# Three depthwise 3x3 convolutions of a four-layer kernel: four taps on TensorE and five on VectorE, in pieces of 448 pixels

## The chip, the core and the metric

The kernel runs on one NeuronCore of a Trainium2 chip. A core has several engines with instruction queues of their own: TensorE (PE, matrix products into the PSUM banks), VectorE (DVE), ScalarE (ACT), GpSimd (POOL) and SyncE (SP, which issues DMA transfers here). [...] SBUF is the working memory with 128 partitions, and PSUM is the memory that TensorE writes to, in banks of 512 fp32 numbers for each partition.

The metric is the device time of one execution in microseconds (us). The time before is 17090.54 us, the median of three runs (17080.33 to 17101.61).

## What is computed

A batch of 4 images of 96 channels and 56 x 56 pixels passes four layers in a row, each with a group norm ahead and a residual around it: attention, a selective scan in eight directions, a top-k aggregation over windows, and a state-space layer in four directions with a convolutional bottleneck. Depthwise 3x3 convolutions occur in three places, one in layer 1 and two in layer 3:

```python
# layer 1, DI = 192 channels
xz = einsum('bchw,dc->bdhw', x, w_in);  xc, z = split(xz, 2, axis=1)
xc = conv_general_dilated(xc, conv_w, (1, 1), 'SAME', feature_group_count=DI)
xc = silu(xc + conv_b)
xs = cross_scan(xc)        # rows, columns, diagonals, antidiagonals, and each reversed

# layer 3, E = 192 channels
xi, z = split(einsum('bchw,oc->bohw', x, in_proj_w), 2, axis=1)
xi = silu(conv2d(xi, conv_w, conv_b, groups=E, pad=1))
...
t = relu(bn(conv2d(u, c1_w, c1_b)))                           # 1x1, 192 -> 384
t = relu(bn(conv2d(t, c2_w, c2_b, groups=2 * E, pad=1)))      # depthwise
t = conv2d(t, c3_w, c3_b)                                     # 1x1, 384 -> 96
s = sigmoid(relu(t.mean((2, 3)) @ se1_w.T + se1_b) @ se2_w.T + se2_b)
return t + t * s
```

A depthwise convolution gives each output pixel as a sum of nine products: nine neighbours of the pixel in its own channel, each by a weight of that channel. One of the nine products, over all pixels of a tile, is called a tap below. Everything is fp32.

## The kernel before

**Tiles.** A map of 56 x 56 has 3136 pixels (`L`), cut into `NCH` = 7 chunks of `CH` = 448 pixels, that is 8 rows. A convolution works on a tile of 128 partitions. In the input stages of layers 1 and 3 a tile holds 64 channels of two images; with `NPAIR` = 2 pairs of images and `NB` = 3 blocks of 64 channels there are 6 tiles in a stage. In the bottleneck a tile holds 128 of the 384 channels of one image, `NM` = 3 tiles for each of the 4 images.

**The convolution before.** `depthwise` (L326 to L333) reads a map with a border of zeros, `xp` or `t1` of 58 x 58, whose border four GpSimd memsets write for every tile (`pad_border`, L319). VectorE runs one scaling (L331) and eight multiply-adds (L333) over all 3136 pixels, one after another, with the sum `cv` in SBUF.

**Layer 1's input, `into_scan` (L252 to L317).** For each pair: load image x (L273, queue SP, one buffer), `group_norm` (L88 to L110: statistics by VectorE, two tiny products by TensorE, a root by ScalarE, the scaling by VectorE), store the normalised image (L276), the same for the second image. Then for each tile j: for each chunk two matmuls, one for each image (L282), and a ScalarE copy into the map (L293); `depthwise`; Silu over the whole tile by ScalarE (L299); a doubled copy `dup` of the tile, one half by ScalarE (L302) and one by GpSimd (L303); four orders of the pixels for the scans: rows (stored as it is, L307), columns (copied by ScalarE, L311), diagonals and antidiagonals (copied by GpSimd, L313 and L315), each stored by SP's queue (L316).

**Layer 3's input, `into_layer3` (L846 to L895).** The same, with two orders only: rows and columns (ScalarE's copy, L888), stored in halves of 64 partitions.

**Layer 3's end, `layer3` (L1246 on).** For each image `gathered` loads the normalised image `xn` (L1285) and, for 7 groups of 448 pixels, the four scan results `y0` to `y3` (L1293 and L1299). VectorE adds them (L1303, L1304) and normalises them (`norm_rows`, L596), multiplies by a matmul's result z (L1309, L1310), and TensorE transposes them (L1314) into `g` (ScalarE's copy, L1318). Then `bottleneck`: for each tile, the c1 matmuls (L1330, two for each chunk), Relu by ScalarE into the map (L1334), `depthwise`, Relu over the whole tile into `t2` (L1341). When all three tiles are there: the c3 matmuls (L1351, three for each chunk), ScalarE's output (L1352) with sums for the mean, the two small products of the gate (L1356 to L1366), and seven output products (L1370, VectorE), each stored by GpSimd's queue (L1371).

**What sets the order.** The tile framework schedules instructions by their dependencies, and each engine runs its own queue in that order. In these three stages nothing is ordered by hand before the change. Other stages (`scans`, `cumulative`) use `in_order` (L52 to L67), which ties every instruction of a block to the one written ahead of it on the same engine. The two pools of an image's gather (`ob`, `os`) are closed before those of its bottleneck (`tb`, `t1`, `ts`) open, so both use the same stretch of SBUF, and a load of the next gather has to wait until whatever lies at its address in the bottleneck has been read for the last time.

Of the kernel before, what the change touches and what calls it, by code (L numbers as in the profile page):

```python
# [9 lines left out]
F32 = mybir.dt.float32  # L10
AF = mybir.ActivationFunctionType
# [20 lines left out]
def view(ap, offset, dims):  # L32

    return bass.AP(ap.tensor, ap.offset + offset, [ap.ap[0], *dims])


def flat(t):
    return t.rearrange("p a b -> p (a b)")
# [31 lines left out]
class Net:  # L70
# [180 lines left out]

    def into_scan(self, xin, dram, orders):  # L252
# [3 lines left out]
        us = []  # L256
        xs = [dram.tile([C, L], F32, name=f"l1x{b}") for b in range(B)]
        with ExitStack() as cx:
# [8 lines left out]
            for pr in range(NPAIR):  # L267
                u = [dram.tile([128, NB, L], F32, name=f"l1u{pr}{o}") for o in orders]
                us.append(dict(zip(orders, u)))
                xn = []  # L270
                for half in range(2):
                    x = s1.tile([C, L], F32, name="x")
                    nc.sync.dma_start(x, xin[2 * pr + half])  # L273
                    xh = s1.tile([C, L], F32, name=f"xn{half}")
                    self.group_norm(x, xh, ss, ps, "p")
                    nc.sync.dma_start(xs[2 * pr + half], xh)  # L276
                    xn.append(xh)

                def project(col, c):
                    p = ps.tile([128, 512], F32, name="p")  # L280
                    for half in range(2):
                        nc.tensor.matmul(  # L282
                            p[64 * half : 64 * half + 64, :CH], win[:, col : col + 64],
                            xn[half][:, c * CH : (c + 1) * CH], start=True, stop=True,
                        )
                    return p

                for j in range(NB):
                    xp = sp.tile([128, H + 2, W + 2], F32, name="xp")
                    self.pad_border(xp)  # L290
                    for c in range(NCH):
                        p = project(64 * j, c)
                        nc.scalar.copy(  # L293
                            xp[:, 1 + 8 * c : 9 + 8 * c, 1 : W + 1],
                            p[:, :CH].rearrange("p (h w) -> p h w", w=W),
                        )
                    cv = sp.tile([128, H, W], F32, name="cv")
                    self.depthwise(cv, xp, cw[:, j, :])
                    nc.scalar.activation(cv, cv, AF.Silu, bias=cb[:, j : j + 1])  # L299

                    dup = sp.tile([128, H, 2 * W], F32, name="dup")
                    nc.scalar.copy(dup[:, :, 0:W], cv)  # L302
                    nc.gpsimd.tensor_copy(dup[:, :, W : 2 * W], cv)  # L303
                    for o in orders:
                        dst = us[pr][o][:, j, :]
                        if o == "rows":
                            nc.sync.dma_start(dst, flat(cv))  # L307
                            continue
                        t = sp.tile([128, W, H], F32, name="t")
                        if o == "cols":  # L310
                            nc.scalar.copy(t, view(cv, 0, [[1, W], [W, H]]))  # L311
                        elif o == "diag":
                            nc.gpsimd.tensor_copy(t, view(dup, 0, [[1, W], [2 * W + 1, H]]))  # L313
                        else:
                            nc.gpsimd.tensor_copy(t, view(dup, W, [[1, W], [2 * W - 1, H]]))  # L315
                        nc.sync.dma_start(dst, flat(t))  # L316
        return us, xs  # L317

    def pad_border(self, xp):  # L319
        nc = self.nc  # L320
        nc.gpsimd.memset(xp[:, 0, :], 0.0)
        nc.gpsimd.memset(xp[:, H + 1, :], 0.0)
        nc.gpsimd.memset(xp[:, 1 : H + 1, 0:1], 0.0)
        nc.gpsimd.memset(xp[:, 1 : H + 1, W + 1 : W + 2], 0.0)

    def depthwise(self, out, xp, w):  # L326
        nc = self.nc
        for k in range(9):
            src = xp[:, k // 3 : k // 3 + H, k % 3 : k % 3 + W]
            if k == 0:  # L330
                nc.vector.tensor_scalar(out, src, w[:, 0:1], None, ALU.mult)  # L331
            else:
                nc.vector.scalar_tensor_tensor(out, src, w[:, k : k + 1], out, ALU.mult, ALU.add)  # L333
# [512 lines left out]
    def into_layer3(self, xin, dram):  # L846
# [4 lines left out]
        with ExitStack() as cx:  # L851
# [8 lines left out]
            for pr in range(NPAIR):  # L860
                xn = []
                for half in range(2):
                    b = 2 * pr + half
                    x = s1.tile([C, L], F32, name="x")
                    nc.sync.dma_start(x, xin[b])
                    xh = s1.tile([C, L], F32, name=f"xn{half}")
                    self.group_norm(x, xh, ss, ps, "p")
                    nc.sync.dma_start(xs[b], xh)
                    xn.append(xh)
                for j in range(NB):  # L870
                    xp = sp.tile([128, H + 2, W + 2], F32, name="xp")
                    self.pad_border(xp)
                    for c in range(NCH):
                        p = ps.tile([128, 512], F32, name="p")
                        for half in range(2):
                            nc.tensor.matmul(
                                p[64 * half : 64 * half + 64, :CH], win[:, 64 * j : 64 * j + 64],
                                xn[half][:, c * CH : (c + 1) * CH], start=True, stop=True,
                            )
                        nc.scalar.copy(  # L880
                            xp[:, 1 + 8 * c : 9 + 8 * c, 1 : W + 1],
                            p[:, :CH].rearrange("p (h w) -> p h w", w=W),
                        )
                    cv = sp.tile([128, H, W], F32, name="cv")
                    self.depthwise(cv, xp, cw[:, j, :])
                    nc.scalar.activation(cv, cv, AF.Silu, bias=cb[:, j : j + 1])
                    t = sp.tile([128, W, H], F32, name="t")
                    nc.scalar.copy(t, view(cv, 0, [[1, W], [W, H]]))  # L888
                    for half in range(2):
                        hs = slice(64 * half, 64 * half + 64)  # L890
                        for o, a in (("rows", cv), ("cols", t)):
                            nc.sync.dma_start(
                                us[o][2 * pr + half, 64 * j : 64 * j + 64, :], flat(a[hs])
                            )
# [350 lines left out]
    def layer3(self, xin, xout, dram):  # L1245
# [4 lines left out]
        with ExitStack() as cx:  # L1250
            wp = cx.enter_context(tc.tile_pool(name="ow", bufs=1))
            ga = cx.enter_context(tc.tile_pool(name="og", bufs=1))
            ps = cx.enter_context(tc.tile_pool(name="op", bufs=4, space=PSUM))
            psz = cx.enter_context(tc.tile_pool(name="oz", bufs=2, space=PSUM))
# [65 lines left out]
            def bottleneck(b, g, sp, s1, ss):  # L1320
# [3 lines left out]
                for m in range(NM):  # L1324
# [200 lines left out]
```

## Time and profile before

| what | us |
|---|---|
| median of 3 runs | 17090.54 |
| profiled execution, device time | 17096.45 |
| its span (first to last instruction on the core) | 17094.7 |
| VectorE busy | 13981.4 (82%) |
| TensorE busy | 13251.9 (78%) |
| ScalarE busy | 12242.0 (72%) |
| GpSimd busy | 7703.0 (45%) |

A profile is one execution, recorded instruction by instruction. These busy shares are averages over stages of different kind: layer 0 runs to about 2619 us, layer 1's input to 2956, its scans and merging and all of layer 2 to 11101, layer 3's input to 11394, its scans to about 16300, and then the four gathers and bottlenecks. How full the engines are where the convolutions run shows only in windows of time.

How to read its lines. A group of instructions: line, engine, operation, output tile <- input tiles, shapes, number | busy us, mean ns of one | idle time of the engine just before them, and what ended it. The chain that ended last is followed back from the last instruction, at each step to what released it, so what is on it sets the time. In a table of windows each row is a stretch of time, with the busy time of each engine and the number of its instructions, then the granted TensorE clock as a share of full speed, and the share of time in which the DMA engines were busy. A timeline gives start and duration of single instructions, and in square brackets how long the engine had been idle and what released it. PEld is TensorE's weight load; a "q" behind an engine's name is its sequencer. A matmul of fp32 numbers shows as two records.

The first half of a convolution in the bottleneck of the last image is short enough to be read through (timeline of TensorE and ScalarE): the c1 matmuls come in one block, and ScalarE follows each chunk.

```profile
16959.02 17.49 PE L1330 MATMUL pn<-g,w_l_c 96*128 96x448 f32 x43
...
16961.93 0.72 ACT L1334 ACTIVATE t<-pn,bn_sh,bn_sc 128x448 f32<-128x448 f32 x1 [2.15 <-PE pn L1330]
...
16963.39 0.73 ACT L1334 ACTIVATE t<-pn,bn_sh,bn_sc 128x448 f32<-128x448 f32 x1 [0.73 <-PE pn L1330]
...
16964.89 0.73 ACT L1334 ACTIVATE t<-pn,bn_sh,bn_sc 128x448 f32<-128x448 f32 x1 [0.78 <-PE pn L1330]
```

### The profile page before, as it was taken

What the parts mean: (1) busy time and instruction counts of PE and PEld (TensorE: products, weight loads), DVE (VectorE), ACT (ScalarE), POOL (GpSimd) and SP (SyncE); (2) the same over time, 40 slices, a digit from 0 to 9 for tenths busy, and PEclk for the clock granted to TensorE, in tenths of its full rate; (3) what the DMA queues carried; (4) which work ended last, traced back from release to release, by engine and by line L of the source; (5) the groups of instructions that cost most, each with busy time, mean ns of one, the idle gap of its engine ahead of it and who ended that gap; (6) DMA issues with size and microseconds to landing.
All of it is one profiled execution on the core that took longest, in us unless ns stands there. A gap on an engine that the chain in (4) does not pass through costs nothing.

```text
span 17094.7 us, 498049 instructions
## 1 busy us (share of the span) xinstructions
PE 13251.9 (78%) x220632; PEld 8905.3 (52%) x220632; DVE 13981.4 (82%) x13756; ACT 12242.0 (72%) x16242; POOL 7703.0 (45%) x4069
## 2 busy tenths in 40 slices
PE   8999992777777777777777667838888888888844
PEld 4333430666666666666666444516666656666622
DVE  7271806999999999999999677768888888888887
ACT  0607063999999999999999234438888888888822
POOL 0000002988888888888888000003333333333300
PEclk6969685999999999999999578959999999999966
DMA  0000003343444444334444830032222212212122
GB/s 13 1 1 1 1 20 133 93 96 89 96 103 105 107 97 94 91 91 102 101 107 101 196 79 12 10 82 50 50 50 52 50 49 51 49 49 50 45 64 65
DMA packets 823179, 1152.29 MB, mean 67 GB/s; under 512 B 309360, under 2 KB 731408, under 8 KB 809248
## 3 DMA queue, kind: packets, MB, share of 16 engines
q1 hardware_dynamic: 763680, 1067.42, 25.7%
q10 hardware_dynamic: 53312, 38.55, 1.0%
q8 instruction: 1734, 28.41, 0.7%
q0 software_dynamic: 4032, 14.46, 0.3%
q14 instruction: 421, 3.45, 0.1%
HBM read 842.93 MB, written 277.18 MB: 66 GB/s over the span
## 4 chain that ended last, share of the span: by engine, by line
DVE 35%; PE 25%; ACT 17%; issue 15%; DMA 4%; POOL 2%; SPq 0%; DVEq 0%; ACTq 0%; POOLq 0%
DVE q L463 17%; PE q L1156 6%; DVE pm L186 6%; ACT ht L488 5%; PE s L202 4%; DVE cv L333 3%; ACT e L451 3%; PE acc L223 3%; ACT phi L1104 2%; PE z L1096 2%; DVE w L1144 2%; ACT w L1112 2%; PE t L386 2%; PE y L500 2%; PE t L479 1%
## 5 line engine op out<-in xcount | busy, mean ns | idle before, releaser
L443 POOL TENSOR_TENSOR q<-du,bm 128x1792 f32<-128x1792 f32 x1344 | 5348.8, 4026 | 2.9 <-DMA bm<-bc 2.9
L463 DVE TENSOR_TENSOR_SCAN q<-e,state,q 128x448 f32<-128x448 f32 x4608 | 4873.9, 1121 | 143.7 <-ACT e L451 142.0
L451 ACT ACTIVATE e<-dl,na 128x448 f32<-128x448 f32 x5376 | 3355.4, 640 | 177.2 <-DVE q L463 120.9
L500 PE MATMUL y<-ht,cd 128*32 128x64 f32 x75264 | 1837.2, 225 | 1479.4 <-ACT ht L488 1478.6
L479 PE MATMUL t<-ident,q 128*128 128x128 f32 x18816 | 2610.7, 292 | 93.8 <-issue 77.7
L1156 PE MATMUL q<-w,m 32*32 32x192 f32 x52224 | 2582.7, 348 | 116.3 <-DVE phi L1165 67.8
L479 PEld LDWEIGHTS t<-ident,q 128*128 128x128 f32 x18816 | 2377.1, 203 | 324.9 <-issue 202.1
L488 ACT COPY ht<-t 128x896 f32<-128x896 f32 x2688 | 2428.3, 903 | 88.9 <-PE t L479 59.5
L500 PEld LDWEIGHTS y<-ht,cd 128*32 128x32 f32 x75264 | 1399.8, 110 | 1956.2 <-ACT ht L488 1942.2
L1156 PEld LDWEIGHTS q<-w,m 32*32 32x32 f32 x52224 | 1876.4, 113 | 733.9 <-issue 163.3
L1165 DVE TENSOR_TENSOR phi<-q,phi 128x768 f32<-128x768 f32 x1632 | 1512.4, 951 | 549.7 <-PE q L1156 535.4
L1177 POOL TENSOR_TENSOR t<-t 128x384 f32<-128x384 f32 x408 | 407.2, 998 | 3002.5 <-DVE t L1176 2996.4
L218 ACT ACTIVATE e<-s 128x448 f32<-128x448 f32 (+1 forms) x2100 | 975.8, 549 | 1055.3 <-PE s L202 1025.2
L1096 PE MATMUL z<-ad,sm 32*32 32x256 f32 x39168 | 1278.5, 391 | 396.9 <-ACT phi L1104 382.7
L1104 ACT COPY phi<-z 128x1536 f32<-128x1536 f32 x816 | 1164.5, 1427 | 538.9 <-PE z L1096 538.9
L1144 DVE TENSOR_TENSOR w<-w,misc 128x3072 f32<-128x3072 f32 x408 | 1364.8, 3345 | 83.6 <-PE misc L1128 46.3
L1112 ACT ACTIVATE w<-phi,lntiny,w_k_rmask 128x3072 f32<-128x3072 f32 x408 | 1203.1, 2949 | 2.6
L186 DVE TENSOR_REDUCE pm<-s 128x2 f32<-128x896 f32 (+1 forms) x1050 | 1075.1, 1084 | 117.2 <-PE s L181 117.2
L1120 ACT ACTIVATE phi<-phi,w_k_nmask 128x3072 f32<-128x3072 f32 x408 | 1165.5, 2857 | 2.4
L181 PE MATMUL s<-ka,qa 32*128 32x448 f32 (+1 forms) x4200 | 1087.5, 922 | 22.2 <-POOL ka L174 17.6
L1096 PEld LDWEIGHTS z<-ad,sm 32*32 32x32 f32 x39168 | 709.0, 105 | 659.8 <-ACT phi L1104 466.6
L230 DVE COPY a<-acc 128x448 f32<-128x448 f32 x21 | 13.1, 624 | 997.5 <-PE acc L223 997.5
(250 smaller groups left out, 17464.3 us busy)
## 6 DMA issues: line engine op xcount, KB each, us to landing
bm<-bc SPq DMA_DIRECT2D x896, 448.0 KB
cm<-cd SPq DMA_DIRECT2D x544, 186.0 KB
l1y<-out SPq DMA_DIRECT2D x672, 96.0 KB
l1y<-out SPq DMA_DIRECT2D x672, 72.0 KB
y<-l1y ACTq DMA_DIRECT2D x224, 168.0 KB
l3y<-y SPq DMA_DIRECT2D x1616, 23.2 KB
w<-l3cr SPq DMA_DIRECT2D x408, 48.0 KB
l3cr<-phi SPq DMA_DIRECT2D x408, 48.0 KB
```

The costliest lines, as they stand in the source:

```text
L186: nc.vector.tensor_reduce(pm[:nq, 2 * i : 2 * i + 2, kc], two[i][:nq, :, :CH], AX.X, ALU.max)
L443: nc.gpsimd.tensor_tensor(q, spread(s["du"][:, j, :], ng), s["bm"][g], ALU.mult)
L451: nc.scalar.activation(e[:, :CH], s["dl"][:, j, :], AF.Exp, scale=na[:, s["k"], j, n : n + 1])
L463: nc.vector.tensor_tensor_scan(a, e, a, first, ALU.mult, ALU.add)
L479: nc.tensor.transpose(flat(t)[:, 128 * c : 128 * c + 128], view(q, h * NC2 + c, [[NC, 128]]), self.ident,)
L488: nc.scalar.copy(t, flat(s["t", j, g, h])[:, : NC2 * 128])
L500: nc.tensor.matmul(s["y", j][r : r + 32, c // 4, 64 * half : 64 * half + 64], s["cd"][:, half, g, c, :], s["t", j, g, h][:, 128 * i + 64 * ...
L1096: nc.tensor.matmul(z[32 * b : 32 * b + 32, p, dh].rearrange("p n d -> p (n d)"), s["s"][ps_, dh, b, lo : lo + 32], st["ad"][ps_, dh, 8 * h ...
L1112: nc.scalar.activation(w.rearrange("p a n d -> p (a n d)"), st["phi"].rearrange("p a b n d -> p (a b n d)"), AF.Sigmoid, bias=lntiny, scal ...
L1144: nc.vector.tensor_tensor(st["w"], st["w"], ut, ALU.mult)
L1156: nc.tensor.matmul(qp[bs, n, :DI], st["m"][bs, 4 * q + n, :], st["w"][bs, :, 4 * q + n, :], start=True, stop=True,)
L1165: nc.vector.tensor_tensor(ph, view(st[q], 0, [[256, 4], [32, 6], [1, 32]]), ph, ALU.mult)
```

## The change

All three convolutions go through a new function `convolve`. It works by chunks of 448 pixels in a PSUM bank. Four of the nine taps become matmuls on TensorE: the weights of tap k stand on the diagonal of a 128 x 128 matrix `dg[:, k, :]`, which VectorE makes from the identity, and the matmul of this matrix with the shifted map adds the tap into the bank. VectorE adds the other five taps in the same bank, in place (input and output in PSUM, second input the map in SBUF). The loop runs one tile ahead: in the pass in which tile j-1 is convolved chunk by chunk, tile j's map is filled chunk by chunk (the input projection and its copy, or c1 and its Relu). The two padded maps are made once for a stage (once for an image in the bottleneck).

```python
def convolve(self, tiles, two, sp, ps):
    nc = self.nc
    on_pe = 4
    for j in range(len(tiles) + 1):
        now = tiles[j] if j < len(tiles) else None
        old = tiles[j - 1] if j > 0 else None
        if now is not None:
            now["xp"] = two[j % 2]
            dg = now["dg"] = sp.tile([128, on_pe, 128], F32, name="dg")
            for k in range(on_pe):
                nc.vector.tensor_scalar(
                    dg[:, k, :], self.ident, now["weights"][:, k : k + 1], None, ALU.mult
                )
        for c in range(NCH):
            if old is not None:
                xp, w = old["xp"], old["weights"]

                def tap(k):
                    y = 8 * c + k // 3
                    return xp[:, y : y + 8, k % 3 : k % 3 + W]

                p = ps.tile([128, 512], F32, name="d")
                q = p[:, :CH].rearrange("p (h w) -> p h w", w=W)
                for k in range(on_pe):
                    nc.tensor.matmul(q, old["dg"][:, k, :], tap(k), start=k == 0, stop=k == on_pe - 1)
            if now is not None:
                now["fill"](c, now["xp"][:, 1 + 8 * c : 9 + 8 * c, 1 : W + 1])
            if old is not None:
                for k in range(on_pe, 9):
                    nc.vector.scalar_tensor_tensor(q, tap(k), w[:, k : k + 1], q, ALU.mult, ALU.add)
                old["ended"](c, q)
```

Around it, stage by stage:

- All three stages put the loop under `in_order`, so the written order holds on every engine.
- Layer 1's input: the four images are loaded at once, two from SP's queue and two from ScalarE's, and normalised in place, all four ahead of the loop. Silu reads each chunk from its bank. The column copy is cut into 7 parts and runs one tile later, between the chunks of the next tile. Both halves of `dup` are now copied by GpSimd, and `dup` has one buffer where it had two; `t` has three where it had two.
- Layer 3's input: the same, without `dup` and the diagonals.
- The bottleneck: Relu of each chunk from its bank into `t2`. The sums `cv` and the second buffer of the maps leave the pool `tb`, and the two maps lie in pool `t1`. The c3 matmuls and all that follows are written after the loop, as before. PSUM: the general pool has 3 banks where it had 4, the pool of z half of what it had, and three banks are new for the convolution.

```diff
+            two = self.padded(s1)
+            xn = []
+            for b in range(B):
+                x = s1.tile([C, L], F32, name=f"xn{b}")
+                (nc.sync if b % 2 == 0 else nc.scalar).dma_start(x, xin[b])
+                xn.append(x)
+
+            def normalise(b):
+                self.group_norm(xn[b], xn[b], ss, ps, "p")
+                nc.sync.dma_start(xs[b], xn[b])
...
-                    self.depthwise(cv, xp, cw[:, j, :])
-                    nc.scalar.activation(cv, cv, AF.Silu, bias=cb[:, j : j + 1])
-
-                    dup = sp.tile([128, H, 2 * W], F32, name="dup")
-                    nc.scalar.copy(dup[:, :, 0:W], cv)
+                    nc.scalar.activation(
+                        kept["cv"][:, 8 * c : 8 * c + 8, :], p, AF.Silu, bias=cb[:, j : j + 1]
+                    )
+                    if last:
+                        last[0]((c,))
+                    if c < NCH - 1:
+                        return
+                    cv = kept["cv"]
+                    nc.sync.dma_start(us[pr]["rows"][:, j, :], flat(cv))
+
+                    dup = s1.tile([128, H, 2 * W], F32, name="dup")
+                    nc.gpsimd.tensor_copy(dup[:, :, 0:W], cv)
                     nc.gpsimd.tensor_copy(dup[:, :, W : 2 * W], cv)
...
+            with in_order(tc):
+                last = []
+                for b in range(B):
+                    normalise(b)
+                self.convolve([tile_of(pr, j) for pr in range(NPAIR) for j in range(NB)], two, sp, ps)
+                last[0](tuple(range(NCH)))
...
-            ps = cx.enter_context(tc.tile_pool(name="op", bufs=4, space=PSUM))
-            psz = cx.enter_context(tc.tile_pool(name="oz", bufs=2, space=PSUM))
+            ps = cx.enter_context(tc.tile_pool(name="op", bufs=3, space=PSUM))
+            psz = cx.enter_context(tc.tile_pool(name="oz", bufs=1, space=PSUM))
+            psd = cx.enter_context(tc.tile_pool(name="od", bufs=3, space=PSUM))
...
-                    cv = sp.tile([128, H, W], F32, name="cv")
-                    self.depthwise(cv, t1, c2[:, m, :])
-                    nc.scalar.activation(
-                        t2[:, m, :].rearrange("p (h w) -> p h w", w=W), cv,
-                        AF.Relu, bias=s2h[:, m : m + 1], scale=s2c[:, m : m + 1],
-                    )
+
+                    def ended(c, p):
+                        nc.scalar.activation(
+                            t2[:, m, c * CH : (c + 1) * CH], flat(p),
+                            AF.Relu, bias=s2h[:, m : m + 1], scale=s2c[:, m : m + 1],
+                        )
+
+                    return dict(weights=c2[:, m, :], fill=fill, ended=ended)
+
+                two = self.padded(s1)
+                with in_order(tc):
+                    self.convolve([tile_of(m) for m in range(NM)], two, sp, psd)
```

## The prediction

> **What bounds it now.** Read the chain over the whole run first: the convolutions are a small share of the end.
>
> ```profile
> DVE q L463 17%; PE q L1156 6%; DVE pm L186 6%; ACT ht L488 5%; PE s L202 4%; DVE cv L333 3%; ACT e L451 3%; PE acc L223 3%; ACT phi L1104 2%; PE z L1096 2%; DVE w L1144 2%; ACT w L1112 2%; PE t L386 2%; PE y L500 2%; PE t L479 1%
> ```
>
> 3% of 17095 us is 510 us, and that is all the edit can shorten. The groups, shapes apart, price the instructions:
>
> ```profile
> L333 DVE SCALAR_TENSOR_TENSOR cv<-xp,w_l_cw,cv 128x3136 f32<-128x3136 f32 x96 | 361.0, 3798 | 1.8
> L333 DVE SCALAR_TENSOR_TENSOR cv<-t,w_l_c,cv 128x3136 f32<-128x3136 f32 x96 | 331.3, 3482 | 2.9 <-DVE cv L333 0.5
> L1330 PE MATMUL pn<-g,w_l_c 96*128 96x448 f32 x336 | 145.5, 598 | 131.3 <-ACT t L1334 131.3
> L248 DVE SCALAR_TENSOR_TENSOR xo<-misc,w_l_bo,xc 96x448 f32<-96x448 f32 x28 | 19.0, 680 | 117.8 <-PE misc L243 117.8
> ```
>
> One tap over a map is 3.48 us undisturbed; L248 has the form of the new taps, one input in PSUM, 448 columns: 0.680. Then the stages by window: layer 1's input, layer 3's input, one bottleneck image, the gather behind it.
>
> ```profile
> core 0: us, PE busy (x) PEld busy (x) DVE busy (x) ACT busy (x) POOL busy (x), PEclk, DMA share, GB/s
> 2619.00:2956.00 337.00, 52.92 (x184) 21.71 (x184) 249.41 (x106) 99.71 (x70) 103.55 (x42) 0.55 0.37 144
> 11101.00:11394.00 293.00, 54.80 (x184) 22.79 (x184) 202.58 (x109) 83.25 (x64) 3.14 (x25) 0.55 0.41 100
> 16573.00:16691.00 118.00, 57.21 (x135) 26.61 (x134) 89.08 (x28) 29.39 (x39) 1.24 (x12) 0.73 0.11 25
> 16691.00:16765.00 74.00, 26.63 (x108) 22.94 (x109) 65.44 (x149) 11.35 (x24) 3.58 (x7) 0.55 0.53 140
> ```
>
> In the first three VectorE has most of the time and TensorE is idle and half clocked (0.55). The chain inside layer 1's input:
>
> ```profile
> 2685.79 30.64 DVE cv L333 x9
> ...
> 2933.55 6.16 ACT t L311
> 2939.72 5.13 DMA l1u1cols<-t
> 2945.00 5.57 POOL t L315
> 2950.59 5.07 DMA l1u1anti<-t
> ```
>
> Nine taps in a row are the chain; a tail of copies and stores ends the stage. In layer 1 the taps are also stretched (timelines of VectorE and GpSimd):
>
> ```profile
> 2722.83 8.46 DVE L333 SCALAR_TENSOR_TENSOR cv<-xp,w_l_cw,cv 128x3136 f32<-128x3136 f32 x1
> ```
>
> ```profile
> 2719.23 8.77 POOL L313 COPY t<-dup 128x3136 f32<-128x3136 f32 x1
> ```
>
> Last, the timeline between two images: the next gather's loads (L1285 and those behind it) go out beside this image's tail, and its first sum comes 11.7 later.
>
> ```profile
> 16677.70 0.32 SPq L1285 DMA_DIRECT2D xn<-l3x  x1
> ...
> 16689.38 0.96 DVE L1303 TENSOR_TENSOR y<-y,y 112x768 f32<-112x768 f32 x1 [14.79 <-DMA y<-l3y]
> ```
>
> [...] No tap with a PSUM input runs beside a GpSimd copy here[...]. [...] Here, c3's matmuls start at 16677.7 at 0.75 us a record and run at 0.376 after 16681.1. [...] Here 7 x 0.680 = 4.76 against 3.48, so cutting a tap into seven costs 1.28 us, 0.21 a piece.
>
> **The change, priced.** A full fp32 matmul of 448 columns is two records, 0.75 us warm. A chunk of 448 pixels now asks:
> - TensorE: four diagonals, 3.0, and the next tile's fill: 0.75 in the input stages (two 64-column halves, seen together at 0.75), 1.5 in the bottleneck. Sum 3.75 or 4.5.
> - VectorE: five taps. Dependent taps now start 3.52 apart for 3.48 of work, so 0.04 is added: 5 x 0.72 = 3.6 less an overlap of 0.08 at the bank's change: 3.52. L812, a scaled identity of 112x112, takes 0.278, so four diagonals are about 1.0 a tile: 7 x 3.52 + 1.0 = 25.6 a tile.
> - ScalarE: fill 0.53 (L293), Silu from PSUM about 0.63 (L1352's form), a seventh of the column copy about 1.0: 2.2. It gains nothing and bounds nothing.
> - GpSimd, layer 1, a tile: 2 x 2.8 (L303, now also the half that ScalarE did) + 2 x 5.6 = 16.8.
>
> So TensorE sets the pace by a hair: 7 x 3.75 = 26.25 a tile, against VectorE's 25.6. Before, a tile took 1.84 + 8 x 3.52 = 30.0 without contention, and fill and the wait for it besides.
>
> Unknown: a tap that reads and writes the same bank. From below 0.60 ([...]nothing excludes a small gain), from above 0.85 with a longer write-to-read gap; I take 0.68, L248's own. Four diagonals per tile may wait for a GpSimd copy: 0 to 2.8 each tile, 14 over five tiles; I take 0, since all but one would fall into VectorE's slack.
>
> *Layer 1's input.* Starts at 2621.1 as now. All four loads are out at once; the first two take 11 (10.98 seen beside other transfers): 2632. Four norms in a row, 9.7 + 3 x 8.3: 2666.7. First fill, seven copies: 2670.7 (4 after TensorE's start). Five tiles at 26.25: 131.3. The last tile has no fill, VectorE bounds: 3.0 + 24.6 = 27.6; end 2829.5. Tail: Silu 0.65, two halves 5.6, diagonal and antidiagonal 11.3, store 5.1: 2852.5. Now the stage ends at 2955.8. Gain 103. What is late next is GpSimd's tail, which had been half hidden.
>
> *Layer 3's input.* 11103.8 + 11 + 34.7 of norms and 4 of fill: 11153.5. Then 158.9 as above: 11312.3. Tail: Silu 0.65, last column copy and its queue 8.4, stores 11.6 (l3ucols takes 11.63 now): 11333 against 11393.8. Gain 61. The four loads ahead cost nothing: SP and ScalarE queues are empty then.
>
> *Bottleneck.* An image now takes 117 from the first c1 matmul to the last c3 output. New: first fill 11.9[...], two iterations of 7 x 4.5 = 31.5, then the third. TensorE's order there is 24 diagonals, one c3 matmul, the last four diagonals, and the other 20 of c3. The 24 run ahead of VectorE by three banks, so they end after 3 + 4 x 3.52 = 17.1; the 25 matmuls behind them take 18.8; 0.8 for the last output. VectorE's own last tile and its Relu, 3 + 24.6 + 0.6, end inside these 35.9. Sum 11.9 + 63.0 + 17.1 + 18.8 + 0.8 = 111.6. Gain 5.4 x 4 = 22.
>
> But memory moves too. Now the gather's buffers lie over maps and accumulators that are free when the last tap ends, so loads go out at 16677.70. In the changed layout xn and the y tiles lie over x and t2, which the last output product and c3 still read. SP's queue holds xn's load first, and everything behind it waits. So: c3's end, + 10.1 to the last product (the last image's own time: 17076.0 to 17086.2), + 11.7 loads (16677.70 to 16689.38), + 12.6 first group, + 49.3 and 1.9 for the six others and the transposes: 85.6 where 75.0 stand now. Loss 10.6 x 3 = 32. (z's single buffer adds nothing: its four matmuls, free to run after L1310, have VectorE's next 8 us of sums and norms as cover. If that cover failed it would be 1 to 2 us a group, 7 groups, 4 images.) The three general banks of c3 and c1 are covered by the diagonals between them. The bottleneck loses 10 net.
>
> Sum: 103 + 61 + 22 - 32 = 154. The profiled execution took 17096.45 (its span 17094.7), so 16942; it lies 6 above the median shown, 17090.54. For a median that is 16936, given as 16940.
>
> **Rivals.**
> A. VectorE bounds. If a tap in a bank takes 0.80 start to start plus banks' waits, a chunk is 4.12: 84 chunks of the input stages x 0.37 = 31, diagonals no longer covered 10, last tiles of the bottleneck 28 x 0.6 = 17: 58 lost, some 16995. For it: each tap waits for the one before in the same bank. Against: L248's 679 to 680 with PSUM input.
> B. The gather is not held: loads overlap as now, because the first groups' other buffers are free. Then 32 comes back: some 16905. Against: a queue in order.
> C. Slower. The one mechanism is the tap's read-modify-write in a bank: at a start-to-start time of 0.98 a chunk is 4.9, the input stages lose 84 x 1.15 + 10, the bottleneck 56 x 0.4 + 28 x 1.38: 168, and the gain of 154 is gone. At 1.04 it gives 17155. No row of the trace is near: it would need 40% over L248[...].
> D. No change: a part of C or a TensorE at a granted clock near 0.77 (3.75 becomes 4.9); in these windows it was 0.55, but with idle time between matmuls, and 0.89 where L282 ran densely.
>
> **Chances and range.** Main, 16895 to 16990: 0.60. A: 0.21. B: 0.07. D: 0.05. C: 0.07. Beyond 0.2% (34 us, about what a measurement here can tell from no change): faster 0.88, same 0.05, slower 0.07. The range runs from 16885 (a tap at 0.60 saves only in last tiles, with B) to 17020 (A with the diagonals' 14).
>
> **What would show it.** Right: the 448-pixel taps at 680 ns with least and greatest close together while GpSimd copies; diagonals' records at 0.376; 26 us a tile; windows near 232 and 229 us; from one image's first c1 matmul to the next 197; the load of xn after the last product of the image before. Wrong: taps above 0.75, idle TensorE waiting for VectorE's banks, a granted clock under 0.9 inside the loops, or xn's load beside c3.

## The result, and the profile after

The changed kernel took 16967.32 us, the median of 4 runs (16951.1 to 16983.67), against 17094.62 for the kernel before, measured beside it. The ratio is 0.9927, with a 95% interval from 0.9909 to 0.9944. The forecast was 16940 with a range from 16885 to 17020 and a chance of 0.88 for faster: right in direction, in size a little too high. The profiled execution gained 121.8 us of span (17094.7 to 16972.9). Where it came from, part by part, read from the chains and timelines of the two traces:

| part | before | after | gain | forecast |
|---|---|---|---|---|
| layer 1's input: first load of x to the end of the last store | 334.5 | 246.9 | 87.6 | 103 |
| layer 3's input: the same | 289.8 | 241.7 | 48.1 | 61 |
| first c1 matmul to the end, four images | 713.1 | 730.5 | -17.4 | -10 |
| everything else, unchanged in code | | | 3.5 | 0 |

The windows of the changed kernel: layer 1's input, layer 3's input, the second image's bottleneck, the gather behind it, and last the loop of layer 1 alone.

```profile
core 0: us, PE busy (x) PEld busy (x) DVE busy (x) ACT busy (x) POOL busy (x), PEclk, DMA share, GB/s
2619.00:2867.00 248.00, 176.27 (x520) 73.14 (x520) 175.16 (x286) 89.37 (x132) 102.68 (x32) 0.84 0.51 195
11015.00:11258.00 243.00, 177.41 (x520) 73.72 (x520) 175.36 (x288) 88.24 (x132) 0.86 (x9) 0.85 0.45 119
16442.00:16555.00 113.00, 111.77 (x295) 54.69 (x294) 72.92 (x111) 35.44 (x56) 0.33 (x4) 0.99 0.05 11
16555.00:16641.00 86.00, 28.76 (x109) 24.73 (x108) 67.16 (x151) 10.92 (x23) 3.58 (x7) 0.54 0.55 140
2668.00:2812.00 144.00, 144.00 (x424) 57.01 (x420) 120.58 (x187) 64.08 (x98) 68.05 (x16) 1.00 0.40 168
```

The last row shows the loop as forecast: TensorE is busy in all of its 144 us at full clock, VectorE in 120.6. TensorE is the bound. The row ahead of it shows the cost: 86 us and more between an image's c3 and the next c1 matmul, where 74 to 75 had been (87.4 behind the first image, from the end of its last c3 output).

The chain of layer 1's input in the changed kernel (start, duration, what) begins and ends so:

```profile
2619.80 10.43 DMA xn<-x
...
2660.95 7.53 PE p L332 x28
2668.48 3.20 PE d L290 x8
2672.59 3.20 PE d L290 x8
...
2843.61 2.80 POOL dup L364
2846.47 11.30 POOL t L367 x2
2857.79 0.32 SPq L370
2858.20 8.49 DMA l1u1cols<-t
```

The taps have left the chain inside the loop (those of the last tile, which has no fill beside it, are still on it), and the diagonals of L290 are on it in their place, one group every 4.11 us. That spacing is the first thing that differs from the forecast, which had 3.75. The taps themselves (groups of one line, with least, median and greatest duration in ns):

```profile
L295 DVE SCALAR_TENSOR_TENSOR d<-xp,w_l_cw,d x420: 680/690/692, 2671.8 to 11235.1; 128x448 f32<-128x448 f32 x140
L295 DVE SCALAR_TENSOR_TENSOR d<-xp,w_l_c,d x420: 681/690/691, 16256.2 to 16943.7; 128x448 f32<-128x448 f32 x140
```

690 ns where 680 had been taken, with 12 ns between least and greatest, though GpSimd was busy for 68 us of layer 1's loop.

### The profile page after: what moved, and what is told of

Same layout as the page of the kernel before. It is cut to its first block, busy times and chain, and to the rows that moved or that the text cites. A ratio compares the mean times of both kernels' runs of the same rounds, so it can differ in the third digit from the quotient of the medians.

```text
span 16972.9 us, 501799 instructions
## 1 busy us (share of the span) xinstructions
PE 13744.0 (81%) x221976; PEld 9147.0 (54%) x221976; DVE 13830.2 (81%) x14476; ACT 12262.4 (72%) x16444; POOL 7699.5 (45%) x4027
## 3 DMA queue, kind: packets, MB, share of 16 engines
q14 instruction: 430, 3.52, 0.1%
## 4 chain that ended last, share of the span: by engine, by line
DVE 29%; PE 26%; issue 20%; ACT 16%; POOL 5%; DMA 3%; SPq 0%; POOLq 0%; DVEq 0%; ACTq 0%
DVE q L511 16%; DVE pm L186 6%; ACT ht L536 5%; PE q L1230 4%; PE s L202 4%; ACT e L499 3%; PE d L290 3%; PE acc L223 3%; PE y L548 2%; PE t L527 2%; PE t L434 2%; PE z L1170 1%; ACT phi L1178 1%; DVE w L1218 1%; POOL m L1210 1%
## 5 line engine op out<-in xcount | busy, mean ns | idle before, releaser
L1218 DVE TENSOR_TENSOR w<-w,misc 128x3072 f32<-128x3072 f32 x408 | 1365.3, 3346 | 85.6 <-PE misc L1202 48.2
L1170 PEld LDWEIGHTS z<-ad,sm 32*32 32x32 f32 x39168 | 711.1, 105 | 661.6 <-ACT phi L1178 468.0
L230 DVE COPY a<-acc 128x448 f32<-128x448 f32 x21 | 13.1, 625 | 999.4 <-PE acc L223 999.4
```

The costliest lines, as they stand in the source:

```text
L1170: nc.tensor.matmul(z[32 * b : 32 * b + 32, p, dh].rearrange("p n d -> p (n d)"), s["s"][ps_, dh, b, lo : lo + 32], st["ad"][ps_, dh, 8 * h ...
L1218: nc.vector.tensor_tensor(st["w"], st["w"], ut, ALU.mult)
```

## The experiments

Each experiment edits the changed kernel. Small effects are read from the stretch of the trace that they concern, because runs of one kernel spread over some 30 us; from trace to trace, the stages that no edit touches differ by 16 to 23 us each.

### Why a chunk takes 4.11 us and not 3.75

Timeline of TensorE in the changed kernel, layer 1's loop, then the bottleneck's:

```profile
2672.52 3.27 PE L290 MATMUL d<-xp,dg 128*128 128x448 f32 x8
2675.72 0.97 PE L332 MATMUL p<-xn,w_l_win 96*64 96x448 f32 x4
...
16257.44 3.17 PE L290 MATMUL d<-xp,dg 128*128 128x448 f32 x8
16260.45 1.67 PE L1404 MATMUL pn<-g,w_l_c 96*128 96x448 f32 x4
```

From start to start the bottleneck's eight records of four diagonals take 3.01 us and its fill 1.51, as forecast. In layer 1 the same eight records take 3.20 and the fill 0.90, where 0.75 was expected. The fill there works on 64 columns of the array, two images side by side. The theory: TensorE loses time at each change between the whole array and the 64-column halves. Two runs test it.

*Fewer changes* (run e2_block4).

```diff
-                if now is not None:
-                    now["fill"](c, now["xp"][:, 1 + 8 * c : 9 + 8 * c, 1 : W + 1])
+                at = c // 4 * 4
+                if now is not None and c == min(at + 4, NCH) - 1:
+                    for f in range(at, c + 1):
+                        now["fill"](f, now["xp"][:, 1 + 8 * f : 9 + 8 * f, 1 : W + 1])
```

> The changed kernel, with the fills put out in two blocks a tile (chunks 0 to 3, then 4 to 6) where there was one fill for each chunk; no work is left out. Theory (TensorE loses 0.36 us for each pair of switches between the diagonals' full array and the fills' 64-column halves): an input-stage tile falls from 28.75 to 7 x 3.75 + 2 x 0.36 = 27.0 us, each input stage is 9 us shorter, the total 18 less; the bottleneck, where fill and diagonal have the same array, keeps 31.5 a tile. Rival (the 0.36 belongs to each fill, or is a wait for a bank that ScalarE releases): 28.75 a tile or longer, no gain.

```profile
2679.32 3.23 PE L334 MATMUL p<-xn,w_l_win 96*64 96x448 f32 x16
2682.47 9.29 PE L290 MATMUL d<-xp,dg 128*128 128x448 f32 x24
2691.69 2.48 PE L334 MATMUL p<-xn,w_l_win 96*64 96x448 f32 x12
2694.10 12.29 PE L290 MATMUL d<-xp,dg 128*128 128x448 f32 x32
2706.32 0.97 PE L334 MATMUL p<-xn,w_l_win 96*64 96x448 f32 x4
```

Between the first and the last of these starts lies one tile: 27.0 us, as the theory said, against 7 x 4.107 = 28.75. The two input stages took 238.2 and 231.5 us, 8.7 and 10.2 less. The median, 16967.63, doesn't show it. In the profiled run the scans and layer 2 between the two stages took 4.9 more, and the part from the first c1 matmul 6.4 more (736.9 against 730.5), where the blocks save no change of shape. The blocks need not be the cause of that: the next run has the changed kernel's bottleneck without blocks and took 736.2 there. Most of the difference is in the four first fills, 12.7 to 13.1 us each where the changed kernel's trace has 10.7 to 12.4.

*No change of shape at all* (e3_wide). Weights with zeros in the other image's half make each fill two matmuls over the whole array.

```diff
-                            p[64 * half : 64 * half + 64, :CH], win[:, 64 * j : 64 * j + 64],
-                            xn[2 * pr + half][:, c * CH : (c + 1) * CH], start=True, stop=True,
+                            p[:, :CH], wide[:, 2 * j + half, :],
+                            xn[2 * pr + half][:, c * CH : (c + 1) * CH], start=half == 0, stop=half == 1,
```

> The changed kernel, with the fills of the input stages as two matmuls over all 128 columns (weights of the one image zero in the other's half) that add up in the bank, in place of two 64-column halves; the added zeros change no value. Theory (the 0.36 comes from changing the array's shape): no switch is left, a chunk is 3.0 + 1.5 = 4.51 us as in the bottleneck, a tile 31.6, each input stage 14 longer, the total 28 more. Rival (the 0.36 belongs to the fill or to a bank): 4.87 a chunk, 34.1 a tile, the total 53 more.

```profile
2670.99 1.67 PE L339 MATMUL p<-xn,wide 96*128 96x448 f32 x4
2672.49 3.17 PE L290 MATMUL d<-xp,dg 128*128 128x448 f32 x8
2675.51 0.92 PE L339 MATMUL p<-xn,wide 96*128 96x448 f32 x2
```

A chunk takes 4.52 us (2670.99 to 2675.51), and the diagonals are back at 3.02. The rival's 4.87 falls. The time of a single run was 17015.45. Each stage was 18 to 19 longer than in the changed kernel, 14.2 of it by 35 chunks of 0.41; in layer 1 the first fill, whose two matmuls for a chunk no longer run side by side (in the loop the four records take 1.50 us, where the halves took 0.90), took 12.5 in place of 7.5. So a pair of changes costs 0.36 us, and a wait for a bank has no part in it.

### Which engine bounds, and by how much

`on_pe = 3` in place of 4, everywhere (e8_pe3).

> The changed kernel with three taps on TensorE and six on VectorE. Theory (TensorE bounds the loops by a small margin, VectorE is just behind): VectorE bounds at 6 x 0.718 = 4.31 a chunk and 31.0 a tile with its three diagonals, against 28.75 in the input stages and 31.5 in the bottleneck; the last tile of each loop takes 30 where it took 25; each input stage 16 longer, the total 40 to 50 more, some 17010. Rival (VectorE has much slack, TensorE alone is short): 3.36 a chunk and a gain.

The input stages took 258.0 and 251.4 us, 11 and 10 more than the changed kernel, where 16 were expected. The steady chunk takes 4.22 us and TensorE now waits in each (timeline of TensorE):

```profile
2714.39 2.52 PE L290 MATMUL d<-xp,dg 128*128 128x448 f32 x6 [0.79 <-ACT cv L352]
2716.84 0.97 PE L332 MATMUL p<-xn,w_l_win 96*64 96x448 f32 x4
2718.61 0.64 PE L290 MATMUL d<-xp,dg 128*128 128x448 f32 x1 [0.79 <-ACT cv L352]
```

The bank it waits for is freed by Silu, which waits for the sixth tap: VectorE bounds, by 4.22 against 4.11. "TensorE by a small margin" holds. The total of a single run, 16981.58, was far under the 17010 expected, because the bottleneck became faster: its first image takes 107 us, against 111.4. With four taps TensorE bounds more clearly there, since a c1 fill costs 1.51. With a diagonal less the next chunk starts after 3.77 us and not 4.51, and the two tiles with fills take 54.6 us where they took 63.1. VectorE falls behind meanwhile, and the last tile with c3 takes 40.0 where it took 37.7.

### Are the taps spared by GpSimd because the sum lies in PSUM?

The theory: the sum in PSUM is what spares them, since with both inputs in SBUF a tap of before took 8.46 us beside a copy and 3.48 without. The five taps of VectorE summed in SBUF (e7_sbuf):

```diff
+                    acc = sp.tile([128, 8, W], F32, name="acc")
                     for k in range(on_pe, 9):
-                        nc.vector.scalar_tensor_tensor(q, tap(k), w[:, k : k + 1], q, ALU.mult, ALU.add)
-                    old["ended"](c, q)
+                        nc.vector.scalar_tensor_tensor(
+                            acc, tap(k), w[:, k : k + 1], q if k == on_pe else acc, ALU.mult, ALU.add
+                        )
+                    old["ended"](c, acc)
```

> The changed kernel with the five VectorE taps summed in SBUF: the first reads the bank and the map, the other four read two SBUF tiles, and Silu or Relu read SBUF. Theory [...]: in layer 1, where GpSimd copies 16.8 us a tile, some taps take over 2 us and the stage grows by 10 to 30; in layer 3's input, where GpSimd is idle, every tap stays under 0.70 and the stage within 2 us of the changed kernel. Rival (the taps are undisturbed because they are short or ordered): greatest durations as now, 0.69, in both stages.

Layer 1's input took 306.3 us, 59 more than the changed kernel; layer 3's 240.7, one less, with no tap above 0.687 (a single run, 17033.10 in all). The groups of that kernel (least, median and greatest ns), then VectorE and GpSimd at one place:

```profile
L296 DVE SCALAR_TENSOR_TENSOR acc<-xp,w_l_cw,acc x336: 683/685/6051, 2673.5 to 11294.9; 128x448 f32<-128x448 f32 x168
...
L296 DVE SCALAR_TENSOR_TENSOR acc<-xp,w_l_cw,d x84: 667/676/682, 2672.7 to 11292.0; 128x448 f32<-128x448 f32 x84
```

```profile
2701.59 0.67 DVE L296 SCALAR_TENSOR_TENSOR acc<-xp,w_l_cw,d 128x448 f32<-128x448 f32 x1
2702.37 17.77 DVE L296 SCALAR_TENSOR_TENSOR acc<-xp,w_l_cw,acc 128x448 f32<-128x448 f32 x4
2720.07 0.67 DVE L296 SCALAR_TENSOR_TENSOR acc<-xp,w_l_cw,d 128x448 f32<-128x448 f32 x1
2720.77 2.85 DVE L296 SCALAR_TENSOR_TENSOR acc<-xp,w_l_cw,acc 128x448 f32<-128x448 f32 x4
```

```profile
2701.66 2.80 POOL L366 COPY dup<-cv 128x3136 f32<-128x3136 f32 x1 [79.88 <-ACT cv L355]
2704.39 3.20 POOL L367 COPY dup<-cv 128x3136 f32<-128x3136 f32 x1
2707.65 12.01 POOL L370 COPY t<-dup 128x3136 f32<-128x3136 f32 x2
```

Four taps with both inputs in SBUF take 17.77 us beside four GpSimd copies, and 2.85 right after them; a tap with one input in PSUM is never above 0.682 in the input stages. In the changed kernel, where GpSimd is busy with copies for 16.98 of the 17.05 us from 2700.76 to 2717.81, no tap is above 0.692. The trace of before had no such tap beside a copy; these two have. The size was underestimated by half or more: four taps beside four copies took about as long as the copies (17.77 us, against 18.0), so a short tap can wait for about a whole one (6.05 at most, beside copies of about 6.0).

### The bottleneck: what the images gain and what the gather loses

Putting back the bottleneck of before alone (e4_oldbottle):

> The changed input stages of layers 1 and 3, with the bottleneck of the kernel before (nine taps on VectorE, its pools and banks). Theory (the bottleneck's own gain is smaller than what its memory layout costs the next gather): from the first c1 matmul to the end 713 us as before the change, where the changed kernel has 730.5, so 17 us faster than the changed kernel, about 16950. Rival (the changed bottleneck is worth its shorter images): slower than the changed kernel by about 20.

The median was 16952.48 (ratio to before 0.9912, interval 0.9899 to 0.9926), 15 less than the changed kernel, and in the trace the part from the first c1 matmul to the end took 711.1 us. So the new bottleneck, as placed, is a small loss: 19 us by these two traces, and the same code took 736.2 in e3_wide. The medians alone would not settle 15 us, since their intervals overlap; the stretch of the traces does. The cause, in the changed kernel's timelines of VectorE and SP's queue:

```profile
16363.33 0.68 DVE L1449 SCALAR_TENSOR_TENSOR o<-t,gate,x 96x448 f32<-96x448 f32 x1 [0.91 <-DMA out<-o]
16374.82 0.96 DVE L1378 TENSOR_TENSOR y<-y,y 112x768 f32<-112x768 f32 x1 [10.81 <-PE z L1384]
```

```profile
16364.15 0.31 SPq L1360 DMA_DIRECT2D xn<-l3x  x1
```

The load of the next gather goes out 0.14 us after the last output product ends, and VectorE stands still until it has come. The forecast, and the account of the kernel before ahead of it, put this down to the bytes: xn and the y tiles would lie over x and t2. The first run moved the bytes (e1_gap).

```diff
+                two = self.padded(s1)
+                gap = s1.tile([128, 5120], F32, name="gap")
+                nc.gpsimd.memset(gap[:, 0:1], 0.0)
                 x = s1.tile([C, L], F32, name="x")
...
-                two = self.padded(s1)
```

> The changed kernel, with the two padded maps of the bottleneck placed ahead of x and t2 in their pool and 20 KB of a partition left empty behind them, so that the next gather's buffers lie over the maps and the empty stretch and no longer over x and t2. Theory (the gather is held up by what lies at its address): the load of xn goes out beside c3 instead of after the last output product, the stretch from the last c3 output to the next image's first c1 matmul falls from 87 to 75 to 78 us, the period of an image from 198.8/200.6/199.8 to about 188 to 190, and the total by 30, to about 16937. Rival (the gather is slower because z has one buffer and the general banks are three): the load goes out earlier, but the stretch stays above 85 and the total the same.

Neither came true. At new addresses (by the order and sizes of the tiles in the kernel), over maps that are free, the load still waits for the last product (same two views):

```profile
16384.69 0.68 DVE L1451 SCALAR_TENSOR_TENSOR o<-t,gate,x 96x448 f32<-96x448 f32 x1 [0.87 <-DMA out<-o]
16396.40 0.96 DVE L1378 TENSOR_TENSOR y<-y,y 112x768 f32<-112x768 f32 x1 [11.03 <-DMA y<-l3y]
```

```profile
16385.51 0.31 SPq L1360 DMA_DIRECT2D xn<-l3x  x1
```

The median was 16971.73. What is left in common is the pool: the maps share one with x and t3, which the last product reads. The new theory, that a tile waits for the last use of every tile in the old pool that its memory came from, is tested by the same addresses in two pools (e5_pool).

```diff
+                    mp = c2x.enter_context(tc.tile_pool(name="tm", bufs=1))
                     s1 = c2x.enter_context(tc.tile_pool(name="t1", bufs=1))
...
-                two = self.padded(s1)
-                gap = s1.tile([128, 5120], F32, name="gap")
+                two = self.padded(mp)
+                gap = mp.tile([128, 5120], F32, name="gap")
```

> As e1_gap, at the same addresses, but the two maps and the empty stretch are a pool of their own, opened ahead of the pool that holds x and t2. Theory formed after e1_gap (a new tile waits for the last use of every tile in the old pool that its memory came from, not of the bytes at its address): the load of xn goes out within 1 us of the last tap, some 19 us earlier against c3's end than in the changed kernel; the first sum follows 11.7 later, and with the seven output products between the gather's sums the stretch from c3's end to the next c1 matmul falls from 87 to about 73, 43 less over three images, some 16925 in all. Rival (the loads are late for another reason, such as SP's queue or the order the scheduler chose): the load still follows the last output product and the total is the changed kernel's.

```profile
16327.83 1.42 DVE L295 SCALAR_TENSOR_TENSOR d<-xp,w_l_c,d 128x448 f32<-128x448 f32 x2
16340.41 0.96 DVE L1378 TENSOR_TENSOR y<-y,y 112x768 f32<-112x768 f32 x1 [11.15 <-DMA y<-l3y]
...
16351.73 1.87 DVE L1451 SCALAR_TENSOR_TENSOR o<-t,gate,x 96x448 f32<-96x448 f32 x3 [3.93 <-DMA out<-o]
```

```profile
16329.41 0.31 SPq L1360 DMA_DIRECT2D xn<-l3x  x1
```

The load goes out 0.16 us after the last tap. The median was 16932.32 (ratio 0.9907, interval 0.9892 to 0.9922), 35 less than the changed kernel; its interval overlaps the changed kernel's, but the part from the first c1 matmul to the end took 705.7 us in place of 730.5. An image's period, from its first c1 matmul to the next image's, is 190.9 to 191.6 us, where it had been 198.8 to 200.6. The gain is 8 to 10 a period and not the 14 expected (the gather takes 77.7 us, where 73 was forecast), and the VectorE lines show why: its queue is in order, the output products sit between the gather's sums, and some of them wait for one of three buffers that a store has to free. The waits sum to 23.1 us in nine places.

### Together

With the blocks of fills added (e6_pool_block4):

> e5_pool with the fills in two blocks a tile as in e2_block4. Theory (both losses are independent): 18 less than e5_pool, about 16905, and faster than the changed kernel beyond the interval. Rival (one of them moves the end elsewhere): no faster than the better of the two alone.

16920.27, 12 less than e5_pool in the same series, where 18 were forecast; ratio 0.9899 (0.9883 to 0.9916), which still overlaps the changed kernel's. Then `bufs=NCH` for the output product (e9_o7):

> e6_pool_block4 with seven buffers for the output product in place of three. Theory (with the loads let loose, VectorE waits inside the gather for the output's stores, which now queue beside the gather's loads): the waits of VectorE for a store vanish (e5_pool shows 23.1 us in nine of them), an image's period falls from 191 to 185 to 187, the total by 12 to 18. Rival (the gather's loads bound that stretch anyway): period and total unchanged.

The waits for stores are gone, the seven products run in one block of 4.26 us, and the periods are 181.5, 183.4 and 180.9. The part from the first c1 matmul took 672.8 us in place of 705.6, some 7 of this in shorter first fills. The medians don't show that gain: 16912.71 is 8 less than e6_pool_block4's, but in another series, and against the kernel before in their own series both gained 171. Its runs lie between 16894 and 16929, and the profiled one was the fastest.

Three taps on TensorE in the bottleneck, kept with the blocks, gave nothing (e10_pe3):

> e9_o7 with three taps on TensorE in the bottleneck only, four elsewhere. Theory from e8_pe3 (in the bottleneck TensorE also has c1 and c3, so a tap more on VectorE shortens an image by 4 to 6 us): the period falls by 4 to 6, the total by 16 to 22. Rival (e8_pe3's images were shorter because the gather was held up otherwise): no change.

16909.89, and periods of 188 to 191: the theory failed. An image took 112 us there, not 107 (VectorE's taps in the first image and the gather behind it):

```profile
L296 DVE SCALAR_TENSOR_TENSOR d<-xp,w_l_c,d 128x448 f32<-128x448 f32 x126 | 85.2, 689 | 24.1 <-PE d L289 20.1
```

Of these 20.1 us of waiting for diagonals, 15.7 go by during the first fill, as in e12_mix below (15.8); the other 4.4 come later, where diagonals stand behind c1 fills in a row. The gather, too, became longer, 75.5 us where e9_o7 had 70.2. The last tap is what lets its loads go, and with a tap more on VectorE it ends nearer to the end of the image: xn's load goes out 9.7 us ahead of c3's end in e9_o7, and 3.1 ahead here. Moving half of the norms behind the first fill, on top of that (e11_norm):

> e10_pe3 with the norms of images 2 and 3 moved behind the first tile's fill. Theory (the four norms in a row leave TensorE idle for 31 us ahead of each input stage, and VectorE is idle during the first fill): each input stage is about 7 us shorter, the total 14 less. Rival (VectorE is the bound of the loop by then and pays the norms back): no change or slower.

16921.78, no gain. The input stages fell by 1.9 and 2.8 us and not by 7. The rival was right about the size but layer 1's trace shows another cause, since TensorE waits for nothing inside the loop. The first fill ends 9 us before the diagonals start, because the two late norms' small products stand between them in TensorE's queue and wait for VectorE's statistics (the diagonals start 44.5 us after the first load, in place of 48.6), and the first 32 records then take 14.55 us in place of 12.29. Last, the blocks where the array's shape changes and nowhere else (e12_mix):

> e10_pe3 with the fills in two blocks only in the input stages; in the bottleneck three taps on TensorE and one fill for each chunk, as in e8_pe3. Theory (e8_pe3's images took 107 us from the first c1 matmul to c3's end and e10_pe3's 112 because the blocks starved VectorE, which waits 20 us for diagonals there): 107 us an image, a period of 178 to 183, 4 to 8 a period less than e10_pe3, the total 16885 to 16905. Rival (the image is bound by c3 behind the last tap whatever the blocks): 112 an image and e10_pe3's total.

Windows of that kernel: an image, and the gather behind it.

```profile
16214.24:16321.50 107.26, 99.60 (x254) 46.49 (x252) 85.53 (x129) 34.33 (x58) 0.78 (x9) 0.98 0.02 4
16321.50:16397.77 76.27, 30.38 (x116) 26.48 (x117) 68.05 (x156) 11.47 (x25) 3.61 (x7) 0.52 0.65 170
```

107.26 + 76.27 = 183.5 us a period. The median was 16888.49 (16873.17 to 16912.09; ratio to before 0.9886, interval 0.9870 to 0.9903), faster than both kernels, and its interval lies clear of the changed kernel's. That it is faster than e9_o7 is not shown: the intervals overlap, and from the first c1 matmul to the end its trace has 675.4 us against 672.8. The image is shorter (107 against 111 to 113) and the gather longer (76 against 70), since xn's load goes out only 2.3 us ahead of c3's end.

## Why the prediction was right, and where it was off

- **The bound after the change.** Right: TensorE at full clock, VectorE a little behind, shown by the loop's window and by the run with three taps.
- **The tap's price.** Right: 0.690 for the 0.680 taken from L248, 3.49 us for a chunk of five in the last tile of layer 1 where 3.52 stood. Rival A (a dear tap) and rival C (a tap of 0.98 and over) fall, and so does D, with a granted clock of 1.00 in the loop. That GpSimd would not stretch it was assumed, with no trace behind it, and is now shown (0.692 at most). The diagonals, for which 0 to 2.8 us of waiting for a copy had been left open, took 0.272 to 0.283 each; in the trace of before a scaling by VectorE (L110) had taken 7.44 us beside a copy and 1.91 without.
- **"TensorE: four diagonals, 3.0, and the next tile's fill: 0.75": the mis-sized term.** A fill with its two changes of array shape costs 1.11, so a chunk is 4.107, a loop of 35 chunks 143.7 us in place of 131.3. That is 12.4 in each input stage, of the 15 and 13 by which their gains fell short. The 0.75 was right for fills in a row, as in before; it was priced alone and used in alternation.
- **Start and tail of layer 1.** The first fill began 4.4 us sooner after the first load than the sum had it, took 3.5 more, and the tail was 3.6 longer, nearly all in one place: the last store took 8.49 us where 5.1 was used. The sum ended with the store of the antidiagonals; it left out that the last column copy is stored after it in SP's queue, so that two stores run at once (the chain's last lines: L370 at 2857.79, then l1u1cols). With the loop's 12.4 that makes up the 15.
- **The image's own time.** Close, and in part by luck: 111.6 forecast, 111.4 measured for the first image and 111.4 to 113.1 for the others. In the first, the fill took 10.6 where 11.9 was priced, and the last tile's 24 diagonals 18.05 where 17.1 was: at 0.75 each they can't take less than 18 on TensorE, so VectorE's three banks do not set their pace.
- **The gather.** The size was right (85.6 forecast, 87.4 measured behind the first image), and rival B falls. The reason given was only half right. The wait for the last output product is as described, but "lie over x and t2" is not what causes it: moved off them, the load waited as long, and with a pool of its own for the maps it didn't. A period went from 191.4, 192.1 and 194.0 to 198.8, 200.6 and 199.8, a loss of 7.4, 8.5 and 5.8 where 5.2 was forecast. Of the difference the gather's 1.8 is known; the first fill, 10.7 us where the clock granted in its first 4 us was 1.00 and 12.4 where it was 0.57, varies by as much.
- **Signs and readings.** Of the signs, "26 us a tile" (28.75) and windows near 232 and 229 (246.9 and 241.7) failed by the mis-sized term; the others held, with a period of 199 to 201 for the 197. Two readings were loose and nothing rests on them: the third window of before has a clock of 0.73, not 0.55, and the 3% of the chain that L333 has is not all that the edit can shorten, since it takes norms, fills and copies off the chain as well.

The mechanism and its bound were right; the missing 12 us a stage lay in the transition between two pieces of work that were each priced right.

## What to carry to other kernels

When matmuls on the whole array alternate with matmuls on column halves, count the changes (0.36 us a pair here) and batch them. Where both had the same shape, nothing was saved: in the bottleneck, blocks left the image at 113.5 us with four taps on TensorE, and with three, where VectorE sets the pace, they cost 5 us an image (112 against 107) because its diagonals came late. When a pool is rearranged, ask what is last used of everything in the pool whose memory the next stage takes, and put what is free early in a pool of its own. Then whatever ends last among the users of that pool lets the next loads go, so a change that shortens a stage can lengthen the one behind it. Where VectorE works beside GpSimd copies, try a running sum in PSUM: here it kept the taps at 0.692 us or less, where a sum in SBUF let them grow to 6.05.

## What the runs showed of the hardware that was not expected

- A pair of changes between 128-column and 64-column matmuls cost 0.36 us of TensorE time (4.107 against 3.75 a chunk; 27.0 against 28.75 a tile with two pairs in place of seven).
- A 448-pixel tap with both inputs in SBUF took up to 6.05 us beside a GpSimd copy of 128x3136, nine times its 0.685, while the copies were stretched only from 2.80 to 3.20 and from 11.30 to 12.01 for two.
- Taps that depend on one another in one bank start 0.725 apart for 0.690 of work, as close as they had been with the sum in SBUF (3.52 for 3.48).
